# The last bias's product and the weight-quadrant sums of a two-layer graph network, moved behind the first group's first layer

## The chip, the cores and the metric

The kernel runs on one core of a Trainium2 chip. The metric is device time in microseconds (us) for the whole program, and the figure for a kernel is the median of its runs. The engines are named as in the profile: PE is TensorE (PEld are its weight loads), DVE is VectorE, ACT is ScalarE, POOL is GpSimd, and SP is SyncE, which issues the transfers.

## The reference

Two layers stand one behind the other, each with a layer norm and a ReLU in front and a residual around it. The first is a graph attention with one head; its output is half attention, half the plain product h. The second is masked attention with eight heads. Inputs and outputs are fp32. Cut to what is computed:

```python
def _layernorm(x, axis=-1, eps=1e-5):
    m = jnp.mean(x, axis=axis, keepdims=True)
    v = jnp.var(x, axis=axis, keepdims=True)
    return (x - m) / jnp.sqrt(v + eps)

# x: 64 x 256 x 512, adj: 256 x 256, all weights fp32
def layer_0(X, A, W, a):                      # W: 512 x 256, a: 2 x 256 x 1
    h = jnp.einsum('bnf,fo->bno', X, W)
    att_self = jnp.einsum('bno,od->bnd', h, a[0])
    att_neigh = jnp.einsum('bno,od->bnd', h, a[1])
    e = jax.nn.leaky_relu(att_self + jnp.swapaxes(att_neigh, 1, 2), 0.2)
    e = e + -1e9 * (1.0 - A)[None, :, :]
    alpha = jax.nn.softmax(e, axis=-1)
    out = jnp.einsum('bij,bjo->bio', alpha, h)
    return jnp.concatenate([out, h], axis=-1)

def layer_1(h, adj, Wq, bq, Wk, bk, Wv, bv, Wo, bo):   # 8 heads of 64
    q = split_heads(h @ Wq.T + bq)
    k = split_heads(h @ Wk.T + bk)
    v = split_heads(h @ Wv.T + bv)
    scores = jnp.einsum('bhqd,bhkd->bhqk', q, k) / np.sqrt(64)
    scores = jnp.where((adj == 0)[None, None], -jnp.inf, scores)
    attn = jax.nn.softmax(scores, axis=-1)
    out = jnp.einsum('bhqk,bhkd->bhqd', attn, v)       # heads joined again
    return out @ Wo.T + bo

x = x + layer_0(jnp.maximum(_layernorm(x), 0.0), adj, ...)
x = x + layer_1(jnp.maximum(_layernorm(x), 0.0), adj, ...)
```

## The kernel before

The 64 samples go through in 32 groups of two samples, that is four tiles of 128 tokens (GT = 4). Each group passes through three parts: `first_layer` (layer 0, the second norm, and the operands for the projections), `project` (q, k and v), and attention with the output product. The parts are generators, and a driver takes steps of the parts of three groups in turn. All matmuls and transposes are chained into one fixed order on TensorE:

```python
    before = []

    def in_order(instruction):
        if before:
            tc.add_manual_dep(
                instruction.ins, before.pop(),
                mybir.DependencyInfo(mybir.DependencyClass.NoSync, mybir.DependencyReason.DATA),
                reason="TensorE's order",
            )
        before.append(instruction.ins.name)

    def matmul(*args, **kwargs):
        in_order(nc.tensor.matmul(*args, **kwargs))

    def transpose(*args):
        in_order(nc.tensor.transpose(*args))

```

The products with the four weight matrices q, k, v and o are done as seven half-size products instead of eight. For that, sums of quadrants are needed on both sides. Those of the weights are made once, four for each matrix; slot W12 is overwritten by T1.

```python
    def weight_sums(name):
        w = w_sb[name]
        nc.vector.tensor_sub(w[:, :, T3, :], w[:, :, W22, :], w[:, :, W12, :])
        nc.vector.tensor_sub(w[:, :, T1, :], w[:, :, W12, :], w[:, :, W11, :])
        nc.vector.tensor_sub(w[:, :, T2, :], w[:, :, W22, :], w[:, :, T1, :])
        nc.vector.tensor_sub(w[:, :, T4, :], w[:, :, W21, :], w[:, :, T2, :])

    def last_bias():


        pb = mm("pb")
        for q in range(NQ):
            for half in range(2):
                b = small.tile([P, P], F32, tag="power", name=f"bv_{q}_{half}", bufs=1)
                nc.vector.tensor_scalar(b, ones, bv_col[:, half, q : q + 1], None, op0=ALU.mult)
                matmul(
                    pb, b, w_sb["o"][:, half, 2 * q : 2 * q + 2, :],
                    start=(q == 0 and half == 0), stop=(q == NQ - 1 and half == 1),
                )
        nc.vector.tensor_add(b_out, pb, b_out)
```

`last_bias` takes the bias of v through the output product and adds it to bo. Its four blocks b share one buffer. The weights and bias columns of o come in eight transfers each, behind those of q, k and v. The result b_out is added to every group's x at the end of its first layer.

The norm makes the tiles xn, which are kept in two buffers, and TensorE transposes them:

```python
    def norm_T(src, mv, name):


        ve = small.tile([P, GT], F32, tag="ve", name=f"ve{name}")
        nc.vector.tensor_scalar(ve, mv[:, :, 1], EPS, None, op0=ALU.add)
        rstd = small.tile([P, GT], F32, tag="rstd", name=f"rstd{name}")
        nc.gpsimd.tensor_tensor(rstd, ve, rexp, op=ALU.pow)
        xn = {}

        def normed(t):
            xn[t] = att.tile([P, D], F32, tag="xn", name=f"xn{name}_{t}", bufs=2)
            nc.vector.tensor_scalar(
                xn[t], src[:, t, :], mv[:, t, 0:1], rstd[:, t : t + 1],
                op0=ALU.subtract, op1=ALU.mult,
            )

        def put(t, dst):
            if t + 1 < GT:
                normed(t + 1)
            pt = mm(f"pt{name}_{t}").rearrange("p (c t) -> p c t", c=HP)
            for c in range(HP):
                transpose(pt[:, c, :], xn[t][:, c * P : (c + 1) * P], ident)
            nc.scalar.activation(dst, pt, AF.Relu)

        normed(0)
        return put
```

The sums on the side of the data are made by GpSimd:

```python
    def operand_sums(quads, sums):
        a11, a12, a21, a22 = quads
        nc.gpsimd.tensor_add(sums[:, 0], a21, a22)
        nc.gpsimd.tensor_sub(sums[:, 1], sums[:, 0], a11)
        nc.gpsimd.tensor_sub(sums[:, 2], a11, a21)
        nc.gpsimd.tensor_sub(sums[:, 3], a12, sums[:, 1])
```

The first layer, with the marks GAP, of which the third follows the second norm:

```python
    def first_layer(g):

        xt = xs[g]
        mv = small.tile([P, GT, 2], F32, tag="mv", name=f"mv0_{g}")
        for t in range(GT):
            stats(mv, xt, t, f"0_{g}")
        put = norm_T(xt, mv, f"0_{g}")
        yield GAP

        H = big.tile([P, GT, F1 + 3], F32, tag="H", name=f"H_{g}", bufs=1)
        # ... (cut: for each tile, transposes pt, product ph, copy to H, then pn and e)
        yield GAP
        mv = small.tile([P, GT, 2], F32, tag="mv", name=f"mv1_{g}")
        for r in range(GT):
            b, t = divmod(r, NT)
            po = mm(f"po_{g}_{r}")[:, : F1 + 1]
            for kb in range(NT):
                matmul(
                    po, pT[b][:, kb, t * P : (t + 1) * P], H[:, b * NT + kb, 2:],
                    start=(kb == 0), stop=(kb == NT - 1),
                )
            ri = small.tile([P, 1], F32, tag="ri", name=f"ri_{g}_{r}")
            nc.vector.reciprocal(ri, po[:, F1:])
            nc.vector.scalar_tensor_tensor(
                xt[:, r, :F1], po[:, :F1], ri, xt[:, r, :F1], op0=ALU.mult, op1=ALU.add
            )
            stats(mv, xt, r, f"1_{g}")
            yield
        put = norm_T(xt, mv, f"1_{g}")
        yield GAP
        hT = big.tile([P, HP, TOK], F32, tag="hT1", name=f"hT1_{g}")
        for t in range(GT):
            put(t, hT[:, :, t * P : (t + 1) * P])
            if t == GT - 1:
                break
            yield
        sums = big.tile([P, 4, 2, N], F32, tag="sums", name=f"sums_{g}", bufs=1)
        quads = halves(hT, N)
        operand_sums(quads, sums)
        operands[g] = seven(quads, sums)

        for t in range(GT):
            nc.gpsimd.tensor_add(xt[:, t, :], xt[:, t, :], b_out)
        yield


```

`project` makes seven products for each of q, k and v, with a yield behind each; here without the helpers:

```python
            first = blocks(held_bank(turn[0], f"p{name}1_{g}"))
            product(first, 1, True)
            p1 = kept(first, 0, 0)
            yield
            second = blocks(mm(f"p{name}2_{g}"))
            product(second, 2, True)
            nc.vector.tensor_add(part(0, 0), second, p1)
            yield
            product(first, 6, False)
            p16 = kept(first, 0, 1)
            yield
            # ... (cut: products 7, 5, 4 and 3 in the same manner)
```

Product 1 reads the weight slot W11, 2 reads W21, 6 reads T2, 7 reads T3, 5 reads T1, 4 reads T4 and 3 reads W22. On the other side 1 and 2 read hT itself, and 6 reads the sum `sums[:, 1]`.

The start of the program's main part:

```python
    for name in ("q", "k", "v"):
        weight_sums(name)
    last_bias()
    weight_sums("o")
    run(first_layer(0))
    short = first_layer(1) if NG > 1 else none
    for _ in project(0):
        next(short, None)
    run(short)
    verdict = judge()
    # ... (cut: the steady loop over all groups)
```

The kernel has a second program for inputs with other bounds; it isn't run here. `judge` checks those bounds on the side.

Of the kernel before, what the change touches and what calls it, by code (L numbers as in the profile page):

```python
# [26 lines left out]
def two_gnn_layers(tc, *args):  # L27

    nc = tc.nc
    with tc.tile_pool(name="verdict", bufs=1) as pool:
        wrong = pool.tile([1, 1], I32, name="wrong")
        bounded(tc, *args, wrong)
        again = nc.values_load(wrong[0:1, 0:1], min_val=0, max_val=1)
        with tc.If(again > 0):
            tc.strict_bb_all_engine_barrier()
            any_inputs(tc, *args)
# [3 lines left out]
def bounded(  # L43
# [23 lines left out]
    nc = tc.nc  # L67
# [22 lines left out]
    def mm(name):  # L90
        return psum.tile([P, 512], F32, tag="turn", name=name, bufs=5)

    def held_bank(n, name):
        return psum.tile([P, 512], F32, tag=f"held{n}", name=name, bufs=1)


    before = []

    def in_order(instruction):
        if before:  # L100
            tc.add_manual_dep(
                instruction.ins, before.pop(),
                mybir.DependencyInfo(mybir.DependencyClass.NoSync, mybir.DependencyReason.DATA),
                reason="TensorE's order",
            )
        before.append(instruction.ins.name)

    def matmul(*args, **kwargs):
# [4 lines that stand above are left out]
# [52 lines left out]
    W11, W12, W21, W22, T2, T3, T4 = range(7)  # L165
# [30 lines left out]

    def weight_sums(name):
        w = w_sb[name]
        nc.vector.tensor_sub(w[:, :, T3, :], w[:, :, W22, :], w[:, :, W12, :])
        nc.vector.tensor_sub(w[:, :, T1, :], w[:, :, W12, :], w[:, :, W11, :])  # L200
        nc.vector.tensor_sub(w[:, :, T2, :], w[:, :, W22, :], w[:, :, T1, :])
        nc.vector.tensor_sub(w[:, :, T4, :], w[:, :, W21, :], w[:, :, T2, :])
# [14 lines that stand above are left out]
# [114 lines left out]
    GAP = "gap"  # L331
# [6 lines left out]
# [8 lines that stand above are left out]

        def normed(t):
            xn[t] = att.tile([P, D], F32, tag="xn", name=f"xn{name}_{t}", bufs=2)
            nc.vector.tensor_scalar(  # L349
                xn[t], src[:, t, :], mv[:, t, 0:1], rstd[:, t : t + 1],  # L350
                op0=ALU.subtract, op1=ALU.mult,
            )

        def put(t, dst):
            if t + 1 < GT:
# [8 lines that stand above are left out]
# [22 lines left out]
        }  # L386

    operands = {}

    def first_layer(g):  # L390

# [78 lines left out]
    def place(shape, name):  # L470
        tag = places.pop(0)
        return big.tile(shape, F32, tag=tag, name=name, bufs=1), tag
# [4 lines left out]
    def project(g):  # L477
        ops = operands.pop(g)
        for name in ("q", "k", "v"):
            shape = [P, NT, D] if name == "v" else [P, HP, N]  # L480
            dst = {}
            for b in range(GB):
                dst[b], tag = place(shape, f"{name}_{g}_{b}")
                qkv[name, g, b] = dst[b], tag
            turn[0] = 1 - turn[0]

            def blocks(bank):
                return bank.rearrange("p (o n) -> p o n", o=2)

            def product(out, i, start):  # L490
                a, w = ops[i][0], w_sb[name][:, :, ops[i][1], :]
                for o in range(2):
                    cols = slice(o * P, (o + 1) * P)
                    for c in range(2):
                        of, by = (a[:, c, cols], w[:, c, :]) if name == "v" else (w[:, c, cols], a[:, c, :])
                        matmul(
                            out[:, o, :], of, by, start=start and o == c == 0, stop=o == c == 1,
                            skip_group_check=True,
                        )

            def part(b, half):
                if name == "v":
                    return dst[b][:, :, half * D // 2 : (half + 1) * D // 2]
                return dst[b][:, 2 * half : 2 * half + 2, :]

            def take(to, bank, half):
                if name == "v":
                    nc.scalar.copy(to, bank)
                    return
                for o in range(2):  # L510
                    i = 2 * half + o
                    nc.scalar.activation(
                        to[:, o, :], bank[:, o, :], AF.Identity,
                        bias=bcol[name][:, i : i + 1], scale=1.0,
                    )

            def kept(bank, half, i):
                s = att.tile([P, 2, N], F32, tag=f"kept{i}", name=f"kept{i}_{name}_{g}", bufs=1)
                take(s, bank, half)
                return s  # L520
# [4 lines that stand above are left out]
            yield  # L525
            second = blocks(mm(f"p{name}2_{g}"))
            product(second, 2, True)
            nc.vector.tensor_add(part(0, 0), second, p1)
            yield
            product(first, 6, False)  # L530
            p16 = kept(first, 0, 1)
            yield
            second = blocks(held_bank(1 - turn[0], f"p{name}7_{g}"))
            product(second, 7, True)
            p7 = kept(second, 1, 2)
            yield
            product(first, 5, False)
            nc.vector.tensor_add(part(1, 1), first, p7)  # L538
            yield
            product(second, 4, False)  # L540
            nc.vector.tensor_add(part(1, 0), second, p16)
            yield
            product(first, 3, False)
            take(part(0, 1), first, 1)
            yield
# [108 lines left out]
    def run(part):  # L654
        for _ in part:
            pass

    for name in ("q", "k", "v"):
        weight_sums(name)
    last_bias()  # L660
    weight_sums("o")
    run(first_layer(0))
    short = first_layer(1) if NG > 1 else none
    for _ in project(0):
        next(short, None)
    run(short)
    verdict = judge()
# [3 lines left out]
    for g in range(NG):  # L671
        projected = project(g + 1) if g + 1 < NG else none
        short = first_layer(g + 2) if g + 2 < NG else none
        for step, parts in enumerate(steps):
            b, quad = divmod(step, NQ)
            if waiting is not None:
                weigh(*waiting)
                if waiting[2] == NQ - 1:
                    late = outputs(*waiting[:2])
            waiting = (g, b, quad, *scores(g, b, quad))  # L680
            if step == 1 and g + 3 < NG:
                load(g + 3)
            for part in parts:
                if part == "u":
                    next(projected, None)
                elif part == "o":
                    next(late, None)
                elif next(short, GAP) is GAP:
                    next(verdict, None)
        run(projected)  # L690
        run(short)
# [373 lines left out]
```

## Time and profile before

| | |
|---|---|
| time, median of 3 runs | 2705.36 us (2705.27 to 2707.52) |
| span of the profiled run | 2703.6 us |
| busy: PE, DVE, ACT, POOL | 2618.0, 1667.8, 835.2, 1227.2 us |
| first transposes of the first layer | 38.76 us from the span's start |
| first product of q, first group | 69.02 us |
| first scores, first group | 123.28 us |

The page gives each engine's busy time, then the span in 40 slices of 67.6 us with a digit for the busy tenths. The chain of work that ended last is followed back from the last instruction; 89% of it is PE. The views by time give start and length in us, the engine, the line of the kernel, the operation, its output and inputs, and in brackets how long the engine was idle before and what ended that. A line of the kernel may be a helper's: L109 is every matmul, L112 every transpose. Records of matmuls come twice for each fp32 matmul.

### The profile page before, as it was taken

Reading aid. Unit: us, or ns where it says so; the run is one execution under the profiler, and the core shown is the slowest. Engines: PE = TensorE matmul, PEld = TensorE weight load, DVE = VectorE, ACT = ScalarE, POOL = GpSimd, SP = SyncE. Lnnn points to the kernel's source line nnn. Section 1 sums busy time; section 2 is a strip of 40 time slices with the busy share of each in tenths; the row PEclk is TensorE's granted clock in tenths of the full one; section 3 lists DMA queues with packets and bytes.
Section 4 is the critical chain, followed back from the end, with each engine's and each line's share of the span. In section 5 each row is a group of like instructions: output and inputs, shape, how many; then the busy total and the mean of one; then the engine's idle time right before and its main releaser. Section 6 shows DMA issues by size and latency. Waiting matters only on the chain.

```text
span 2703.6 us, 41522 instructions
## 1 busy us (share of the span) xinstructions
PE 2618.0 (97%) x17150; PEld 2121.2 (78%) x17150; DVE 1667.8 (62%) x2558; ACT 835.2 (31%) x1771; POOL 1227.2 (45%) x1004
## 2 busy tenths in 40 slices
PE   4999999999999999999999999999999999999997
PEld 2878888887887888887778878878878888877875
DVE  5466557665666665666656676656666656666554
ACT  2333332333323333323333233323233333233321
POOL 1443445533544534455435445335445344545443
PEclk9999999999999999999999999999999999999999
DMA  5000001010000000000000000000000000000000
GB/s 164 1 13 32 28 32 36 9 36 32 28 32 20 24 36 24 32 32 9 32 32 24 32 24 17 32 32 24 32 17 24 32 25 31 32 12 28 17 16 25
DMA packets 45890, 78.49 MB, mean 29 GB/s; under 512 B 3712, under 2 KB 10624, under 8 KB 45696
## 3 DMA queue, kind: packets, MB, share of 16 engines
q1 hardware_dynamic: 45696, 75.77, 8.1%
q8 instruction: 137, 2.24, 0.3%
q14 instruction: 57, 0.47, 0.1%
HBM read 42.21 MB, written 33.55 MB: 28 GB/s over the span
## 4 chain that ended last, share of the span: by engine, by line
PE 89%; DVE 8%; DMA 1%; POOL 1%; issue 1%; ACT 0%; SPq 0%; DVEq 0%; ACTq 0%; POOLq 0%
PE pq L109 15%; PE pv L109 14%; PE py L109 13%; PE pk L109 13%; PE pr L109 9%; PE ph L109 8%; PE sc L109 7%; PE po L109 4%; PE pt L112 4%; DVE p L567 3%; DVE r L598 2%; PE total L109 2%; DVE k L538 1%; DVE oT L599 1%; PE pn L112 1%
## 5 line engine op out<-in xcount | busy, mean ns | idle before, releaser
L567 DVE TENSOR_TENSOR p<-p,maskT 128x1024 f32<-128x1024 f32 x256 | 398.4, 1588 | 3.2 <-ACT p L566 3.2
L566 ACT ACTIVATE p<-sc 128x512 f32<-128x512 f32 x512 | 264.3, 603 | 378.3 <-PE sc L109 378.3
L568 POOL TENSOR_TENSOR ps<-p 128x512 f32<-128x512 f32 x256 | 365.9, 1445 | 0.0
L622 DVE TENSOR_TENSOR x<-py,x 128x256 f32<-128x256 f32 x448 | 187.6, 419 | 271.4 <-PE py L109 265.7
L598 DVE RECIPROCAL r<-total 128x256 f32<-128x256 f32 x128 | 224.4, 1753 | 194.5 <-PE total L109 194.5
L414 POOL TENSOR_TENSOR x<-H,x 128x256 f32<-128x256 f32 x128 | 87.1, 680 | 464.3 <-ACT H L413 463.1
L109 PE MATMUL py<-wo_sb,o_sums 128*128 128x256 f32 x1024 | 265.3, 383 | 26.3 <-DVE x L622 21.4
L109 PE MATMUL pr<-p,v 128*32 128x256 f32 x4096 | 250.3, 384 | 5.8 <-DVE p L567 5.8
L109 PE MATMUL sc<-q,k 64*128 64x256 f32 x2048 | 255.8, 389 | 0.0
L109 PE MATMUL pq<-sums,wq_sb 128*128 128x256 f32 x1024 | 245.3, 383 | 0.5 <-DVE q L538 0.5
L109 PE MATMUL pk<-sums,wk_sb 128*128 128x256 f32 x1024 | 244.9, 383 | 0.0
L109 PE MATMUL ph<-w_sb,hT 128*128 128x258 f32 x1024 | 244.1, 381 | 0.3 <-ACT hT L360 0.3
L109 PE MATMUL pv<-wv_sb,sums 128*128 128x256 f32 x1024 | 242.3, 380 | 0.0
L109 PEld LDWEIGHTS sc<-q,k 64*128 64x128 f32 x2048 | 187.6, 187 | 69.4 <-issue 52.6
L109 PEld LDWEIGHTS py<-wo_sb,o_sums 128*128 128x128 f32 x1024 | 190.5, 191 | 62.2 <-POOL o_sums L372 37.9
L360 ACT ACTIVATE hT<-pt 128x512 f32<-128x512 f32 x256 | 153.1, 599 | 263.0 <-PE pt L112 262.8
L349 DVE TENSOR_SCALAR xn<-x,mv,rstd 128x512 f32<-128x512 f32 x256 | 224.3, 887 | 8.0 <-PE pt L112 4.2
L371 POOL TENSOR_TENSOR o_sums<-oT 128x256 f32<-128x256 f32 x64 | 106.1, 1658 | 261.9 <-DVE oT L599 261.9
L109 PEld LDWEIGHTS ph<-w_sb,hT 128*128 128x128 f32 x1024 | 194.6, 190 | 28.1 <-ACT hT L360 0.5
L109 PEld LDWEIGHTS pq<-sums,wq_sb 128*128 128x128 f32 x1024 | 189.6, 190 | 34.4 <-issue 9.9
L109 PEld LDWEIGHTS pk<-sums,wk_sb 128*128 128x128 f32 x1024 | 189.8, 190 | 33.5 <-issue 9.9
L109 PEld LDWEIGHTS pr<-p,v 128*32 128x32 f32 x4096 | 121.0, 110 | 110.7 <-issue 37.9
(145 smaller groups left out, 4059.0 us busy)
## 6 DMA issues: line engine op xcount, KB each, us to landing
x<-in_x_dram SPq DMA_DIRECT2D x32, 1024.0 KB, 5.5
out_dram<-x SPq DMA_DIRECT2D x64, 512.0 KB, 2.8
wq_sb<-in_L_gnn_Wq_dram SPq DMA_DIRECT2D x2, 512.0 KB, 12.1
wk_sb<-in_L_gnn_Wk_dram SPq DMA_DIRECT2D x2, 512.0 KB, 12.7
wv_sb<-in_L_gnn_Wv_dram SPq DMA_DIRECT2D x2, 512.0 KB, 11.7
wo_sb<-in_L_gnn_Wo_dram SPq DMA_DIRECT2D x8, 128.0 KB, 3.4
wv_block<-in_L_gnn_Wv_dram SPq DMA_DIRECT2D x4, 256.0 KB, 2.9
wq_block<-in_L_gnn_Wq_dram SPq DMA_DIRECT2D x4, 256.0 KB, 2.8
```

What stands on the lines that cost most here:

```text
L109: in_order(nc.tensor.matmul(*args, **kwargs))
L112: in_order(nc.tensor.transpose(*args))
L349: nc.vector.tensor_scalar(xn[t], src[:, t, :], mv[:, t, 0:1], rstd[:, t : t + 1], op0=ALU.subtract, op1=ALU.mult,)
L360: nc.scalar.activation(dst, pt, AF.Relu)
L371: nc.gpsimd.tensor_add(sums[:, 0], a21, a22)
L414: nc.gpsimd.tensor_add(xt[:, t, F1:], H[:, t, 2 : F1 + 2], xt[:, t, F1:])
L538: nc.vector.tensor_add(part(1, 1), first, p7)
L566: nc.scalar.activation(pair[:, j], sc[j], AF.Exp, scale=scale)
L567: nc.vector.tensor_mul(pair, pair, maskT[:, None, :, :].to_broadcast([P, 2, NT, N]))
L568: nc.gpsimd.tensor_add(ps[:, 2 * i : 2 * i + 2, :], pair[:, :, 0, :], pair[:, :, 1, :])
L598: nc.vector.reciprocal(r, total)
L622: nc.vector.tensor_add(to, out, to)
```

## The change

`last_bias` and the sums for q move from the start of the program to the third GAP of the first group's first layer, that is behind the first tile xn of its second norm. The sums for k, v and o move in among the 21 steps of the first group's projections, behind the second product of q (for k), of k (for v) and of v (for o), at steps 1, 8 and 15. So that the scheduler doesn't draw the sums forward again, the first sum of each set gets an order edge behind a VectorE instruction that is named last: a tile xn of a norm, or the add behind a product 2. It is for having the first layer's work start without the weights of the second layer. What is computed stays the same.

```diff
--- before.py
+++ after.py
@@ -93,16 +93,20 @@
     def held_bank(n, name):
         return psum.tile([P, 512], F32, tag=f"held{n}", name=name, bufs=1)
 
+    def after(instruction, name):
+
+        tc.add_manual_dep(
+            instruction.ins, name,
+            mybir.DependencyInfo(mybir.DependencyClass.NoSync, mybir.DependencyReason.DATA),
+            reason="the engine's order",
+        )
+
 
     before = []
 
     def in_order(instruction):
         if before:
-            tc.add_manual_dep(
-                instruction.ins, before.pop(),
-                mybir.DependencyInfo(mybir.DependencyClass.NoSync, mybir.DependencyReason.DATA),
-                reason="TensorE's order",
-            )
+            after(instruction, before.pop())
         before.append(instruction.ins.name)
 
     def matmul(*args, **kwargs):
@@ -196,7 +200,8 @@
 
     def weight_sums(name):
         w = w_sb[name]
-        nc.vector.tensor_sub(w[:, :, T3, :], w[:, :, W22, :], w[:, :, W12, :])
+        first = nc.vector.tensor_sub(w[:, :, T3, :], w[:, :, W22, :], w[:, :, W12, :])
+        after(first, latest[0])
         nc.vector.tensor_sub(w[:, :, T1, :], w[:, :, W12, :], w[:, :, W11, :])
         nc.vector.tensor_sub(w[:, :, T2, :], w[:, :, W22, :], w[:, :, T1, :])
         nc.vector.tensor_sub(w[:, :, T4, :], w[:, :, W21, :], w[:, :, T2, :])
@@ -346,10 +351,10 @@
 
         def normed(t):
             xn[t] = att.tile([P, D], F32, tag="xn", name=f"xn{name}_{t}", bufs=2)
-            nc.vector.tensor_scalar(
+            latest[0] = nc.vector.tensor_scalar(
                 xn[t], src[:, t, :], mv[:, t, 0:1], rstd[:, t : t + 1],
                 op0=ALU.subtract, op1=ALU.mult,
-            )
+            ).ins.name
 
         def put(t, dst):
             if t + 1 < GT:
@@ -386,6 +391,7 @@
         }
 
     operands = {}
+    latest = [None]
 
     def first_layer(g):
 
@@ -525,7 +531,7 @@
             yield
             second = blocks(mm(f"p{name}2_{g}"))
             product(second, 2, True)
-            nc.vector.tensor_add(part(0, 0), second, p1)
+            latest[0] = nc.vector.tensor_add(part(0, 0), second, p1).ins.name
             yield
             product(first, 6, False)
             p16 = kept(first, 0, 1)
@@ -655,13 +661,16 @@
         for _ in part:
             pass
 
-    for name in ("q", "k", "v"):
-        weight_sums(name)
-    last_bias()
-    weight_sums("o")
-    run(first_layer(0))
+    gaps = 0
+    for part in first_layer(0):
+        gaps += part is GAP
+        if part is GAP and gaps == 3:
+            last_bias()
+            weight_sums("q")
     short = first_layer(1) if NG > 1 else none
-    for _ in project(0):
+    for i, _ in enumerate(project(0)):
+        if i % 7 == 1:
+            weight_sums("kvo"[i // 7])
         next(short, None)
     run(short)
     verdict = judge()
```

## The prediction

> **What bounds the kernel now.** I read the shares of busy time on the page first. TensorE is busy for 97% of the span, and the slices show that it stays so from the second slice to the last but one: only the first slice (67.6 us each) stands at 4 tenths.
>
> ```profile
> PE 2618.0 (97%) x17150; PEld 2121.2 (78%) x17150; DVE 1667.8 (62%) x2558; ACT 835.2 (31%) x1771; POOL 1227.2 (45%) x1004
> ...
> PE   4999999999999999999999999999999999999997
> ```
>
> The change touches only the first 125 us, so the next view is the table of busy time by stretches of that start. Its columns are stretch, length, then busy us (instructions) of each engine, granted TensorE clock, DMA share, GB/s.
>
> ```profile
> 14.50:29.50 15.00, 0.00 (x0) 0.00 (x0) 10.34 (x24) 2.64 (x12) 0.00 (x0) 1.00 0.91 281
> 29.50:39.00 9.50, 8.33 (x10) 2.47 (x11) 3.44 (x7) 0.72 (x2) 0.00 (x0) 1.00 0.77 177
> 39.00:53.00 14.00, 9.67 (x52) 7.94 (x50) 4.28 (x11) 9.22 (x26) 2.71 (x4) 0.99 0.23 69
> 53.00:69.20 16.20, 9.14 (x33) 7.39 (x34) 13.02 (x32) 1.79 (x3) 6.70 (x7) 0.71 0.01 1
> 69.20:123.40 54.20, 53.07 (x255) 45.60 (x255) 26.39 (x49) 17.51 (x39) 16.68 (x16) 0.96 0.00 1
> ```
>
> TensorE does nothing from 14.5 to 29.5, and from 69.2 on, where the projections begin, it has no holes. What fixes the end is therefore when the projections can begin, and everything behind them is a TensorE queue. The timeline says what the hole waits for (start, length, engine, line, what; in brackets the idle time before and what ended it).
>
> ```profile
> 13.80 0.55 DVE L349 TENSOR_SCALAR xn<-x,mv,rstd 128x512 f32<-128x512 f32 x1
> ...
> 29.19 0.29 DVE L211 TENSOR_SCALAR bv<-ones,bv_col 128x128 f32<-128x128 f32 x1 [1.84 <-DMA bv_col<-in_L_gnn_bv_dram]
> 29.53 2.08 PE L109 MATMUL pb<-wo_sb,bv 128*128 128x512 f32 x2 [18.86 <-DMA wo_sb<-in_L_gnn_Wo_dram]
> ...
> 36.90 2.07 PE L109 MATMUL pb<-wo_sb,bv 128*128 128x512 f32 x2 [0.38 <-DVE bv L211]
> ...
> 38.76 1.14 PE L112 MATMUL pt<-ident,xn 128*128 128x128 f32 x8
> 39.01 0.69 DVE L216 TENSOR_TENSOR b_out<-pb,b_out 128x512 f32<-128x512 f32 x1 [1.57 <-PE pb L109]
> ```
>
> The first normalized tile, xn, is there at 14.35 us, but the transposes that want it stand behind pb in TensorE's fixed order, and pb wants the last weights and bias columns, which land at about 29.2 to 29.5. Then pb itself takes until 38.97. That is 24 us in which the first layer is ready and waits.
>
> [...] The stretch 53.0 to 69.2 above has a mean clock of 0.71, and 16 pq matmuls at 69.02 took 5.63 us against 3.72 for 16 of the same form at 125.2. pb's records agree in another way: two of 512 columns take 2.08 us, 1.04 each, where those of 256 columns follow each other by 0.216 us later on (8 in 1.73); that is half speed, though the table prints 1.00 there. [...] The trace shows xn at 66.49 taking 1.57 us, against 0.55, beside a row of GpSimd adds.
>
> **Part one, removed.** With pb gone from the front, the first transposes run at 14.4. I step through the order as built, with durations from before. TensorE has been idle, so I take half speed until about 22 us. The first four transposes run 14.4 to 15.3 (0.88 at half speed). xn of the second tile ends at 16.2, so its transposes run until 17.1. The first ph, 8 matmuls, takes 3.5 at half speed (1.74 at full): 20.6. The third transposes end at 21.5, the second ph at about 23.6, the fourth transposes at 24.05, the last two ph at 27.5, copy of H 0.35, last transpose of pn: 28.3. Before, from the end of pn (49.95) to the first po (53.08) it took 3.13, and from there to xn of the second norm (63.00) 9.92. Nothing on these engines' orders changes in that stretch, so po starts at 31.4 and the second norm's first xn at 41.4. Before it was 63.00: so far 21.6 us are won. ScalarE's waits for the wv_block transfers (2.70 and 2.77 us in the chain before, between 41 and 47.7) fall out too; they are inside this number. The transfers themselves are issued by SyncE in the same order, and wo and bv have long landed by 41.
>
> **Part two, moved: the bias product comes back.** The order as built on VectorE from there is: xn 0, a sum, xn 1, a sum, 0.8 of statistics, a sum, the first bv, the fourth sum, the other three bv, b_out, xn 2, xn 3. In time: 41.4 + 0.55 + 0.72 + 0.53 + 0.72 + 0.75 + 0.72 + 0.3 gives 45.7 for the first pb. The four bv share one buffer, so the ping-pong is as before: from 29.53 to 38.97 it took 9.44 (4 x 2.08 and 3 waits of 0.38), and TensorE is again cold, having had nothing since about 36.6. So pb ends at 55.1, and b_out at 55.8. The transposes of the second norm stand behind pb, and xn 2 and xn 3 behind b_out: two transposes of 0.44 after pb, then xn 2 and xn 3 at 0.6 to 1.6 each, their transposes, and TensorE's own way reaches the first pq at about 58.6. Before, pq followed 6.0 us behind that first xn (63.00 to 69.02); now it is 17.2. Of the 21.6 us, 11.2 are taken back, 10.4 are left.
>
> **Part three, the new chain through GpSimd.** These lines of before show the piece that b_out now controls.
>
> ```profile
> 63.63 4.14 POOL L464 TENSOR_TENSOR x<-x,b_out 128x512 f32<-128x512 f32 x3 [0.66 <-DVE xn L349]
> ...
> 66.49 1.57 DVE L349 TENSOR_SCALAR xn<-x,mv,rstd 128x512 f32<-128x512 f32 x1
> ...
> 70.13 1.45 POOL L371 TENSOR_TENSOR sums<-hT 128x512 f32<-128x512 f32 x1
> 71.54 1.44 POOL L373 TENSOR_TENSOR sums<-hT 128x512 f32<-128x512 f32 x1
> ...
> 72.95 1.26 POOL L372 TENSOR_TENSOR sums<-sums,hT 128x512 f32<-128x512 f32 x1
> ...
> 74.92 1.89 PE L109 MATMUL pq<-sums,wq_sb 128*128 128x256 f32 x8
> ```
>
> As built, GpSimd adds b_out to the four tiles of x ahead of the operand sums. Before, three of the adds ran while TensorE was still at the transposes, because b_out was there at 39.7. Now they start at 55.8: 4 x 1.40 (1.38 each in the line above, a little for contention) until 61.4, then three sums of 1.42 until 65.7. The third product of q (product 6) reads the sum that comes third in GpSimd's order (L372), so it starts at about 65.8. TensorE's own way to it is shorter: from 58.6 two products of 1.74 and a transpose of 0.44, about 62.5 at full clock. So TensorE waits some 3 us, and the third product starts at 65.8 against 75.09 by the chain of waits (the line above has 74.92 by the record of the matmul itself): **9.3 us earlier**.
>
> **Part four, sums among the projections.** Eight of the sixteen sums, those of k and v, fall into VectorE's gaps: k's four take 2.9 us between 62 and 67, needed only by the third product of k some 20 us later; v's four come ahead of e, where VectorE idled 4.31 us before. They cost nothing. Those of o stand in the second group's second norm: one ahead of ve (0.72), one while GpSimd makes rstd (1.03, hidden), one between xn 0 and xn 1 (TensorE has a product of 1.73 there). Before, TensorE waited 1.1 us for that xn; I put 0.8 us on that. Behind it no engine's order differs.
>
> Sum: 9.3 - 0.8 = 8.5 us. 2705.4 - 8.5 = **2696.9 us**, that is 0.3%.
>
> **The rivals.** *The whole hole is won*: from 38.6 to 14.4 is 24 us, 2681. For it speaks that nothing else held the first layer; against it, that pb's 9.4 us of ping-pong stand in the same queue at a place where nothing else is ready for TensorE, and that the clock goes cold. For this to hold, pb would have to run beside po, and its bv are behind the second xn on VectorE. *VectorE becomes the bound among the projections*: if each of the three sets of sums held a product, 3 x 2.9 us would take back 8.7, and the time would be 2705, no change. Against it: VectorE is busy for 26.4 of the 54.2 us, and the sums stand several products ahead of their use. [...] *GpSimd's adds don't hold the product*, if TensorE's own way is the longer: then the third product starts at 62.5 to 64, 11 to 12.5 us earlier, 2694.
>
> **Range and chances.** The middle is my step-by-step sum. Both the start (31.4 for po, plus or minus 2 for the clock) and the chain through b_out (plus or minus 1.5 for contention) are loose, and up to 2 us may come from how the later stages fall. I take 4 to 12.5 us of gain: 2692.9 to 2701.4. Two per cent would be 54 us either way; the whole touched stretch is 125 us and TensorE's later queue is the same, so 0.005 for faster, 0.985 for within, 0.01 for slower.
>
> **What the profile after would show.** Right: first pt near 14.4, po near 31, pb from about 45.7 to 55 at 1.04 us a record, b_out's adds right behind it, the third pq waiting for GpSimd's sums until about 66, the scores' first start near 115 instead of 123.3. Wrong: pb starting well ahead of 45 or taking half as long, the third pq waiting for nothing, or TensorE waits named weight sums in the projections. The number falls if the first layer keeps a wait that I took for gone (ScalarE behind a wv_block transfer), or if the later queue, the same in order, gets waits from another phase of its engines.

## The result, and the profile after

| | before | after |
|---|---|---|
| time, median (6 runs each, same chip) | 2706.44 us | 2699.72 us |
| range of the runs | 2703.82 to 2709.95 | 2698.52 to 2702.35 |
| span of the profiled run | 2703.6 us | 2697.3 us |
| first scores of the first group, profiled run | 123.28 us | 114.88 us |

The ratio is 0.9975 with a 95% interval of 0.9962 to 0.9988: 6.7 us are won, 0.25%. That lies in the predicted range, 1.8 us short of its middle.

The page after, part 1 and the TensorE slices of part 2:

```profile
PE 2620.4 (97%) x17150; PEld 2118.8 (79%) x17150; DVE 1669.7 (62%) x2558; ACT 835.9 (31%) x1771; POOL 1230.0 (46%) x1004
...
PE   5999999999999999999999999999999999999997
```

Only the first digit moved, from 4 to 5 tenths. The same 17150 matmul records stand in a shorter span, and TensorE was busy for 2.4 us longer (2620.4 against 2618.0), although it does the same work. A longer busy time for the same work points at the clock, which comes back below.

The table of busy time by stretches, cut where the stages of after begin (stretch, length, busy us and instructions of PE, PEld, DVE, ACT, POOL, granted clock, DMA share, GB/s):

```profile
14.20:20.50 6.30, 5.53 (x17) 4.29 (x18) 3.13 (x13) 3.72 (x14) 0.00 (x0) 1.00 1.05 387
...
36.90:45.40 8.50, 0.00 (x0) 0.03 (x1) 8.07 (x23) 0.00 (x0) 1.13 (x2) 0.64 0.12 36
45.40:52.80 7.40, 6.26 (x10) 1.91 (x11) 1.62 (x6) 0.00 (x0) 1.01 (x1) 0.72 0.01 2
52.80:63.60 10.80, 6.04 (x36) 4.87 (x34) 9.34 (x9) 5.55 (x13) 10.03 (x7) 0.98 0.16 49
63.60:67.30 3.70, 3.64 (x12) 3.00 (x13) 2.19 (x2) 0.21 (x1) 1.60 (x2) 0.60 0.24 71
```

The old hole at 14.5 to 29.5 is filled with work. The hole of the second norm, 5.45 us before (the wait ahead of the transposes at 63.70), has grown to 8.5 us, from 36.9 to 45.4; in it VectorE (8.07 of 8.50) makes the second norm, the sums of q and the first bias block. Behind it GpSimd is nearly full (10.03 of 10.80), and then the clock is at 0.60. The timeline names the pieces:

```profile
14.23 1.12 PE L116 MATMUL pt<-ident,xn 128*128 128x128 f32 x4 [3.66 <-DVE xn L354]
...
45.40 2.05 PE L113 MATMUL pb<-wo_sb,bv 128*128 128x512 f32 x2 [8.53 <-issue]
...
51.64 1.12 PE L113 MATMUL pb<-wo_sb,bv 128*128 128x512 f32 x2 [0.38 <-DVE bv L216]
...
52.80 0.69 DVE L221 TENSOR_TENSOR b_out<-pb,b_out 128x512 f32<-128x512 f32 x1 [1.22 <-PE pb L113]
...
53.57 5.74 POOL L470 TENSOR_TENSOR x<-x,b_out 128x512 f32<-128x512 f32 x4 [6.29 <-DVE b_out L221]
...
62.17 1.44 POOL L377 TENSOR_TENSOR sums<-sums,hT 128x512 f32<-128x512 f32 x1
...
63.66 3.40 PE L113 MATMUL pq<-sums,wq_sb 128*128 128x256 f32 x8 [3.69 <-POOL sums L377]
...
114.88 2.00 PE L113 MATMUL sc<-q,k 64*128 64x256 f32 x16
```

The same two marks of before, the second norm's first transposes and the first scores (sc):

```profile
63.70 2.89 PE L112 MATMUL pt<-ident,xn 128*128 128x128 f32 x12 [5.45 <-DVE xn L349]
...
123.28 2.00 PE L109 MATMUL sc<-q,k 64*128 64x256 f32 x16
```

Read the changed kernel's lines from below. The third product of q waited 3.69 us for GpSimd's third sum; GpSimd began its row with four adds of b_out at 53.57, released by b_out; b_out waited for pb. That is the chain that was predicted, 2.1 us earlier than predicted. The product itself took 3.40 us, where the same form took 1.89 at 74.92 before.

### The profile page after: what moved, and what is told of

Same layout as the page of the kernel before. It is cut to its first block, busy times and chain, and to the rows that moved or that the text cites. A ratio compares the mean times of both kernels' runs of the same rounds, so it can differ in the third digit from the quotient of the medians.

```text
span 2697.3 us, 41512 instructions
## 1 busy us (share of the span) xinstructions
PE 2620.4 (97%) x17150; PEld 2118.8 (79%) x17150; DVE 1669.7 (62%) x2558; ACT 835.9 (31%) x1771; POOL 1230.0 (46%) x1004
## 4 chain that ended last, share of the span: by engine, by line
PE 89%; DVE 8%; POOL 1%; issue 1%; DMA 0%; ACT 0%; DVEq 0%
PE pq L113 15%; PE pv L113 14%; PE py L113 13%; PE pk L113 13%; PE pr L113 9%; PE ph L113 8%; PE sc L113 7%; PE po L113 4%; PE pt L116 4%; DVE p L573 3%; DVE r L604 2%; PE total L113 2%; DVE k L544 1%; DVE oT L605 1%; PE pn L116 1%
```

## The experiments

Each kernel is the changed one with the edit shown. The start of the first scores, read from its profile, is the finer measure: it closes the stretch that the change touches. For the first four kernels, the kernel before took 2707.89 us on the same chip, for e5 and e7 2706.64.

### e1: the sums moved, the bias product back in front

```diff
+    last_bias()
     gaps = 0
     for part in first_layer(0):
         gaps += part is GAP
         if part is GAP and gaps == 3:
-            last_bias()
             weight_sums("q")
```

> The weight sums stay where the change put them; the bias product goes back to the front of TensorE's order. Theory (the gain is pb's place alone): pb starts again at about 29.5 us and the first transposes at about 38.5, so nothing is won, and the q sums among the second norm and the o sums in the second group's norm cost 1 to 3 us: first scores at 123 to 126 us (before 123.3, after 114.9), time 2706 to 2709. Rival (moving VectorE's 16 sums away from the start brings the gain): first scores near 115, time near 2700.

Measured: 2713.80 us, ratio to before 1.0022 (1.0012 to 1.0031), first scores at 128.9. The timeline of TensorE:

```profile
29.39 2.07 PE L113 MATMUL pb<-wo_sb,bv 128*128 128x512 f32 x2 [18.73 <-DMA wo_sb<-in_L_gnn_Wo_dram]
...
71.50 5.32 PE L113 MATMUL pq<-hT,wq_sb 128*128 128x256 f32 x16
78.68 0.66 PE L116 MATMUL pt<-ident,xn 128*128 128x128 f32 x4 [1.86 <-DVE xn L354]
```

The rival falls: without the move of pb nothing is won, and pb waits for the transfer as before. The first scores came 5.6 us later than before, more than the 1 to 3 expected: 2.5 had gathered by q's first product (71.50 against 69.02). Of these, 1.0 lies ahead of the second norm's first transposes (64.66 against 63.70), where no moved sum stands, and 1.5 in the second norm, where the sums of q stand between the tiles xn. Another 1.8 gathers by q's third product, with a new wait of 1.86 us for the second group's first xn: its statistics came behind the sums of q, so that GpSimd made its rstd behind three of the operand sums (at 76.09), where it stood ahead of them before (67.74, the sums from 70.13). The last 1.3 lies behind that, around the sums of o. The gain is pb's place; the moved sums bring none, and by this trace they cost most of the 5.6 us.

### e2: the bias product moved, the sums of q, k and v back in front

```diff
+    for name in ("q", "k", "v"):
+        weight_sums(name)                 # without the order edge
     ...
         if part is GAP and gaps == 3:
             last_bias()
-            weight_sums("q")
+            weight_sums("o")
-    for i, _ in enumerate(project(0)):
-        if i % 7 == 1:
-            weight_sums("kvo"[i // 7])
+    for _ in project(0):
```

> The bias product stays where the change put it; the sums of q, k and v go back to the front, without the order edges; those of o follow the bias product. Theory: the scheduler finds room for the twelve sums in VectorE's idle time of the first layer (nothing waits for VectorE between 17.8 and 29.3), so the first layer keeps its place within 1 us, pb comes 2 to 3 us earlier because no q sums stand in front of the first bv, and the second group's norm loses its wait for the o sums: first scores at 111 to 113 us against 114.9, time 2696 to 2698. Rival (the sums in front hold the tiles xn, which is why they had to be moved): first transposes still at 14.2, but first po 3 to 8 us later than 31.5, first scores 117 or later, time 2702 or more.

Measured: 2693.38 us, ratio 0.9957 (0.9943 to 0.9970), first scores at 110.9. TensorE's timeline:

```profile
31.42 6.36 PE L113 MATMUL po<-H,e 128*128 128x257 f32 x16 [4.19 <-DVE e L437]
...
43.07 2.05 PE L113 MATMUL pb<-wo_sb,bv 128*128 128x512 f32 x2 [5.29 <-issue]
...
60.86 3.58 PE L113 MATMUL pq<-sums,wq_sb 128*128 128x256 f32 x8 [3.26 <-POOL sums L378]
...
102.09 0.66 PE L116 MATMUL pt<-ident,xn 128*128 128x128 f32 x4 [1.13 <-DVE xn L355]
```

The first po came at 31.42, as in the changed kernel (31.48), though its wait for e had grown from 3.14 to 4.19 us. So the twelve sums in front cost about 1.1 us there, as two sums of v stand ahead of and between the steps of e on VectorE; that po was not later I put down to the clock, since the last transposes ahead of e came 1.1 us earlier (26.28 against 27.40), as in e7 (26.41), where the first two ph took 3.16 and 1.91 us, against 3.65 and 2.35 in the changed kernel. In e3, where they came at 26.19 and no sums stand in front, po began at 30.27. For the rest VectorE has room while TensorE works through the first layer: the rival's 3 to 8 us are not there. pb begins 2.3 us earlier, and the second group's norm waits 1.13 us as before the change, not 2.17. Moving these sums was not needed: in front they cost about 1.1 us, moved they cost more. The time lay below the expected 2696 because the end was also shorter here (see e8 to e10).

### e3: four buffers for the bias blocks

```diff
-                b = small.tile([P, P], F32, tag="power", name=f"bv_{q}_{half}", bufs=1)
+                b = small.tile([P, P], F32, tag="bv", name=f"bv_{q}_{half}", bufs=4)
```

> The changed kernel with four buffers for the bias blocks instead of one, so that pb's four matmuls follow each other. Theory (pb and b_out stand on the path): pb from 45.4 to about 50.6 instead of 52.8, b_out, GpSimd's adds and the third product of q 2.1 us earlier, first scores at about 112.8, time about 2697.6. Rival (pb is hidden, and the path runs beside it through VectorE): no change, first scores 114.9, time 2699.7.

Measured: 2697.18 us, ratio 0.9965 (0.9953 to 0.9977), first scores at 111.4.

```profile
30.27 5.11 PE L113 MATMUL po<-H,e 128*128 128x257 f32 x16 [3.13 <-DVE e L436]
...
43.91 5.09 PE L113 MATMUL pb<-wo_sb,bv 128*128 128x512 f32 x8 [8.53 <-issue]
...
59.88 3.30 PE L113 MATMUL pq<-sums,wq_sb 128*128 128x256 f32 x8 [3.69 <-POOL sums L377]
```

pb's eight records now take 5.1 us, against 7.4 (45.40 to 52.76), and the third product comes 3.8 us earlier. Of these, 1.2 to 1.5 come from an earlier start (po at 30.27 instead of 31.48; I put that down to the clock in the first layer, for in e5 po came at 30.09 and the first two ph took 2.85 and 1.91 us, against 3.65 and 2.35 in the changed kernel), the rest from pb. So pb stands on the path, and the rival falls. The times of e3 and of the changed kernel have overlapping intervals; the verdict rests on the trace.

### e4: the adds of b_out behind the operand sums

```diff
-        operand_sums(quads, sums)
+        last = operand_sums(quads, sums).ins.name      # its last instruction
     ...
         for t in range(GT):
-            nc.gpsimd.tensor_add(xt[:, t, :], xt[:, t, :], b_out)
+            add = nc.gpsimd.tensor_add(xt[:, t, :], xt[:, t, :], b_out)
+            if g == 0:
+                after(add, last)
```

> The changed kernel with one more order edge: the first group's four adds of b_out stand behind GpSimd's operand sums. Theory (GpSimd's adds hold the third product of q, and the wait sends TensorE's clock to half speed): the sums start at about 55.5, the third product at about 59.8 instead of 63.7, at full speed (1.9 us instead of 3.4), xn 2 and xn 3 are free of contention; first scores at 109 to 110.5, time about 2694.5. Rival (TensorE's own way through pb and the transposes is the longer, the adds are hidden): third product at 63 or later, time 2699 to 2700.

Measured: 2697.08 us, ratio 0.9960 (0.9946 to 0.9973), first scores at 113.4. TensorE's timeline, and below it VectorE's:

```profile
60.40 1.99 PE L113 MATMUL pq<-sums,wq_sb 128*128 128x256 f32 x8 [0.75 <-POOL sums L377]
...
69.99 1.99 PE L113 MATMUL pq<-hT,wq_sb 128*128 128x256 f32 x8 [1.52 <-ACT kept_q L520]
...
102.88 1.06 PE L116 MATMUL pt<-ident,xn 128*128 128x128 f32 x4 [2.17 <-DVE xn L354]
```

```profile
59.92 0.97 DVE L203 TENSOR_TENSOR wk_sb<-wk_sb 128x512 f32<-128x512 f32 x1
...
67.01 1.75 DVE L207 TENSOR_TENSOR wk_sb<-wk_sb 128x512 f32<-128x512 f32 x1
```

The chain is right: the third product comes 3.3 us earlier and at full speed, the rival falls. But less reached the first scores (1.5 us) than expected (about 5). A new wait of 1.52 us for ScalarE took its place: the adds now run beside the sums of k on VectorE, which stretch from 0.69 to as much as 1.77 us each, ScalarE stands still for 4.77 us, and its copy of a product comes late. In the changed kernel the sums of k stretched too (up to 1.75 us, beside the operand sums), and VectorE was through them no later, at 68.7 against 68.8 here; TensorE now comes earlier and meets them. That ScalarE waited there for small reductions that stand behind k's sums on VectorE is my reading; the reductions end at 68.89 and ScalarE goes on at 68.91, but no run took them away. And behind the wait of 2.17 us the granted clock was 0.50 (104 to 106), so that the product there took 3.21 us, against 1.89 in the changed kernel.

### e5: the bias product behind the fifth product of q

e3's four buffers, and:

```diff
         if part is GAP and gaps == 3:
-            last_bias()
             weight_sums("q")
     for i, _ in enumerate(project(0)):
         if i % 7 == 1:
             weight_sums("kvo"[i // 7])
+        if i == 4:
+            last_bias()
+            add_bias(xs[0])      # the first group's adds of b_out, taken out of its first layer
```

> The bias product, with four buffers, moves on to behind the fifth of q's products, where TensorE is never idle, and the first group's adds of b_out follow it; the weight sums stay as in the change. Theory (pb and b_out's adds are the path between the second norm and the third product): no idle time of TensorE before pb, first product of q at about 46.5 us instead of 55.9, third product at 52 to 54 instead of 63.7 and without the wait for b_out's adds, pb's 3.5 us at full speed paid within the queue; first scores at 104 to 107, time about 2690. Rival (VectorE's q sums and statistics hold the second norm as long as pb did): first product of q at 52 or later, first scores 110 or more, time 2695 or more.

Measured: 2691.99 us, ratio 0.9945 (0.9932 to 0.9959), first scores at 108.6. The timeline:

```profile
50.69 1.01 POOL L349 TENSOR_TENSOR rstd<-ve,rexp 128x4 f32<-128x4 f32 x1
...
53.28 1.12 PE L116 MATMUL pt<-ident,xn 128*128 128x128 f32 x4 [3.48 <-DVE xn L354]
54.19 3.12 PE L113 MATMUL pq<-sums,wq_sb 128*128 128x256 f32 x8
```

The first product of q comes at 45.94 and the third at 54.19, and pb costs 3.4 us of TensorE's queue at full speed (62.78 to 66.21). The rival falls. The first scores are later than the 104 to 107 expected, because of a wait that I had not seen: the second group's first norm gets its rstd from GpSimd behind three of the operand sums, so its xn held TensorE for 3.48 us, and the clock fell again (3.12 us for the third product, against 1.89 in the kernel before). It is the wait of e1 at 78.68, longer because TensorE comes to it sooner.

### e7: late bias, sums in front

e5's late bias with four buffers, the sums of q, k and v in front as in e2, those of o behind `add_bias`.

> The late bias of the last-named kind together with the sums of q, k and v at the front, as where the bias alone was moved, and those of o behind the late bias. Theory: both savings add up, because they stand at different places of one chain: second norm free of q sums, first product of q at about 45.5, third at 50 to 52, the second group's norm without its o sums (wait of 1.1 instead of 2.2); first scores at 101 to 104, time about 2687. Rival (ScalarE's squares for the bounds, which wait for wv_block transfers, hold the products once they start this early): a TensorE wait named ScalarE of 1 us or more among q's products, first scores 105 or more, time 2690 or more.

Measured: 2685.66 us, ratio 0.9924 (0.9911 to 0.9938), first scores at 103.4. TensorE's timeline, with one line of GpSimd:

```profile
45.09 1.01 POOL L350 TENSOR_TENSOR rstd<-ve,rexp 128x4 f32<-128x4 f32 x1 [2.77 <-DVE ve L348]
46.82 3.78 PE L113 MATMUL pq<-hT,wq_sb 128*128 128x256 f32 x16
...
51.52 1.99 PE L113 MATMUL pq<-sums,wq_sb 128*128 128x256 f32 x8 [0.48 <-POOL sums L378]
...
58.98 3.60 PE L113 MATMUL pb<-wo_sb,bv 128*128 128x512 f32 x8
```

The savings add up, and no wait for ScalarE appears among q's products. In the first scores they do more than add up: e2 brought 4.0 us over the changed kernel, e5 6.3, the two together 11.5. e5's wait of 3.48 us is gone, because without the sums of q in the second norm the second group's rstd is made at 45.09, ahead of the operand sums. So it was the moved sums of q that had put it behind them. This kernel is faster than both: 21.0 us faster than before, where the change brought 6.7.

### e6, e8, e9 and e10: what repeats

In the first pair of profiles the first scores came 8.4 us earlier, but the span was only 6.3 shorter: 2.1 us were lost behind them. e6 and e10 are the changed kernel again, e8 and e9 the kernel before.

> The changed kernel itself, profiled once more, to see what repeats. Theory (the stretch up to the first scores is set by the program, the rest differs by where TensorE's clock falls in the last 100 us): first scores within 2 us of 114.9, third product of q again behind GpSimd's sums, from the first scores to the end again 2580 to 2584 us. Rival (the loss behind the first scores, 2582.4 us against 2580.3 before, belongs to the change): the same 2582.4 within 0.3.

> The kernel before, profiled once more, for the stretch from the first scores to the end, which was 2580.3 us before and 2582.4 and 2582.8 in two profiles of the changed kernel. Theory (that stretch differs by where TensorE's clock falls in the last 100 us, not by the change): a value anywhere from 2580 to 2584, with the time spent at half speed in the last 100 us going with it. Rival (the change itself made it 2.1 us longer): 2580.3 within 0.5 again.

> The same as the run before it, a third profile of the kernel before. Theory: first scores within 3 us of 123.3, from there to the end 2580 to 2584, not the same value as in the other profiles. Rival: 2580.3 within 0.5 for a third time.

> A third profile of the changed kernel. Theory (the window of the clock falls differently each time): first scores between 113 and 118 us, third product of q behind GpSimd's sums after a wait of 3.7, from the first scores to the end 2580 to 2584. Rival (the end is longer by the change): 2582.4 to 2582.8 again.

Measured; the last column is TensorE's busy time at half speed in the last 110 us, added up from the granted clock of stretches of 1 us:

| profile | first scores | from there to the end | busy at half speed |
|---|---|---|---|
| before | 123.28 | 2580.3 | 6.7 |
| before, e8 | 122.91 | 2584.2 | 15.8 |
| before, e9 | 123.85 | 2583.0 | 13.2 |
| after | 114.88 | 2582.4 | 12.7 |
| after, e6 | 117.69 | 2582.8 | 12.6 |
| after, e10 | 117.84 | 2582.8 | 12.9 |

The rival falls by the profiles of before: there the same stretch took up to 2584.2, longer than after. (Those of after alone, 2582.4 to 2582.8, fit the rival as well.) It goes with the time at half speed: take half of the last column from the one before it, and between 2576 and 2577 us remain in all six. (e2, with 6.7 at half speed, took 2580.4.) So the end is the clock's, not the change's; the first profile of before had a short one. The three profiles of before agree on the first scores within 1 us. Those of after don't, and e6 missed its expectation (within 2 us of 114.9). TensorE's timeline of e6 shows why:

```profile
63.51 3.78 PE L113 MATMUL pq<-sums,wq_sb 128*128 128x256 f32 x8 [3.70 <-POOL sums L377]
...
67.94 2.75 PE L113 MATMUL pq<-sums,wq_sb 128*128 128x256 f32 x8
...
107.22 1.11 PE L116 MATMUL pt<-ident,xn 128*128 128x128 f32 x4 [2.17 <-DVE xn L354]
108.12 3.14 PE L113 MATMUL pv<-wv_sb,sums 128*128 128x256 f32 x8
```

The third product starts as in the first profile (63.66), but the half speed behind it reaches into the next product (2.75 us, against 1.89 in the first profile), and the wait of 2.17 us is followed by half speed too (3.14 us for the product behind it), which the first profile was spared (1.89). On the mean of three, the first scores come at 123.3 before and 116.8 after: 6.5 us, which is what the times show (6.7).

## Why the prediction was right, and which term was off

| step | predicted | measured, first profile |
|---|---|---|
| first transposes | 14.4 | 14.23 |
| first po | 31.4 | 31.48 |
| first xn of the second norm | 41.4 | 41.64 |
| pb | 45.7 to 55.1 | 45.40 to 52.76 |
| first product of q | 58.6 | 55.91 |
| third product of q | 65.8 (9.3 won) | 63.66 (11.3 won) |
| half speed behind that wait | nothing | 1.5 (3.1 in e6) |
| sums of o | 0.8 | 1.0 |
| from the wait for these sums to the first scores | as before | 0.3 longer (1.7 in e6, with the clock) |
| first scores, won | 8.5 | 8.4 (e6 and e10 against the mean of before: 5.7 and 5.5) |

That the first profile meets the middle of the forecast is in part luck. There the chain through GpSimd won 11.3 us, 2.0 more than reckoned (the 9.3 count from 75.09 in the chain of waits; from the record at 74.92 they would be 9.1), and the terms that had been left out or reckoned too small took 1.5, 1.0 and 0.3: 8.4 are left, beside the forecast of 8.5. In e6 and e10, where the clock took more, 5.7 and 5.5 are left. The chain and its order were foreseen; that the errors in its sizes cancel was not.

*Part one* held within 0.3 us to the second norm. That half speed would last until about 22 in the first layer was an estimate that no view of before shows, as was the plus or minus 2 us for the clock. It was right: the first ph took 3.65 us, the second 2.35, the third and fourth together 3.65, and in the changed kernel and e3 to e6 the first po came between 30.09 and 31.48. ScalarE's waits for wv_block were indeed gone from the first layer.

*Part two* held in its mechanism, and e3 shows pb on the path. Its size was 2.1 us too large: I carried over the 9.44 us of before, all at half speed, but the second of the four pairs of records took 1.93 us and the last two 1.12 each instead of 2.08, with a mean granted clock of 0.72 (45.4 to 52.8). The 0.72 us that the forecast counts for a weight sum is how they follow each other in before: those of q begin at 18.59, 19.31, 20.04 and 20.76 and take 0.69 us each.

*Part three* held, with the wait for GpSimd 3.69 us where I had about 3; e4 shows that the four adds make it.

The term that was missing is TensorE's clock behind the new waits. I took half speed behind idle time for the first transposes and for pb, and did not ask for it behind a wait of about 3 us that I had just worked out. But that wait was an idle time of 3.7 us, and TensorE came out of it at half speed: the granted clock was 0.50 from 64 to 66. From the third to the fifth product of q, before took 5.64 us (74.92 to 80.56), after 7.14 (63.66 to 70.80), e6 8.76. e4 shows that the wait does it: with 0.75 us in its place the third product took 1.99 us instead of 3.40.

*Part four* was right for k and v within the changed kernel, as no wait named them. The sums of o cost 1.04 us in the wait for the second group's xn. The lines of after, and those of before below them:

```profile
103.66 1.45 POOL L349 TENSOR_TENSOR rstd<-ve,rexp 128x4 f32<-128x4 f32 x1 [3.27 <-DVE mv L341]
105.75 0.66 PE L116 MATMUL pt<-ident,xn 128*128 128x128 f32 x4 [2.17 <-DVE xn L354]
```

```profile
112.82 1.02 POOL L344 TENSOR_TENSOR rstd<-ve,rexp 128x4 f32<-128x4 f32 x1 [2.67 <-DVE ve L342]
114.47 0.66 PE L112 MATMUL pt<-ident,xn 128*128 128x128 f32 x4 [1.13 <-DVE xn L349]
```

About 0.6 of it is the sum ahead of ve, and 0.4 is the sum that I had called hidden: GpSimd's rstd beside it took 1.45 us instead of 1.02. From that transpose to the first scores, before took 8.81 us, after 9.13 with the granted clock at 1.00 throughout, and e6 10.47 with half speed in it (0.84 in the mean). So the clock was missing from this term, too. And "they cost nothing" holds only for that place: e1, e2 and e4 show that moved sums cost as soon as they delay the next norm, stand ahead of the bias blocks, or share the time with GpSimd's adds (this last in my reading of e4).

Of the rivals, the whole hole (24 us) fell as predicted, and e7, with pb and the sums of q out of the second norm, shows that most of it could be had (21.0).

## What to carry to other kernels

Work that is moved from the front of a fixed order comes back wherever it is put. Put it where the bound engine's queue is never empty, not in a stage that waits for other engines anyway: the same product took 7.4 us (5.1 with four buffers) and held a chain of adds in the second norm, and took 3.4 us, with four buffers, among the projections. And when a wait is worked out, ask what the clock does behind it: here a wait of 3.7 us on TensorE cost 1.5 to 3.1 us more after it had ended.

## What the runs showed of the hardware that was not expected

- Beside GpSimd's work, VectorE's tensor_tensor on SBUF took longer in e4, as the tensor_scalar xn did: k's sums took 0.97 to 1.77 us, against 0.69 with GpSimd idle (before, 21.4 to 24.2), and xn 1.49, against 0.54 ahead of GpSimd's sums. GpSimd's own sum took 1.59 there, against 1.27. The prediction had counted it for xn alone.
- A small GpSimd operation took longer, too, beside a tensor_tensor of VectorE: the rstd of the second group's norm, 128x4, took 1.45 us in the first profile of after and 1.46 in e4, where a sum of o (0.66 us) stands beside it, and 1.02 in the first profile of before, where none does.
- The same wait of 2.17 us was followed by half speed in e4, e6 and e10 (3.1 to 3.2 us for the product behind it), and not in the first profile of after, e1, e3 and e5 (1.89); e6, e10 and after are one program. Since the same wait did and did not slow the clock, its length alone doesn't tell.
- The column of the granted clock reads 1.00 in the stretch 14.2 to 20.5, while the records there are those of half speed (8 ph in 3.65 us, 1.91 later). Later it agrees with the durations: 0.60 from 63.6 to 67.3, where eight records of pq took 3.40 us instead of 1.89. So at the start of this trace I go by the durations and not by the column.
